# A graph attention kernel: its last stage compares against a row held in PSUM, spreads destinations by one-row products, and reads stored differences

## The chip, the cores and the metric

The kernel runs on one core of a Trainium2 chip. The metric is device time in microseconds (us), median of several executions. A profile is one execution recorded by the hardware profiler; it names the engines PE (TensorE), DVE (VectorE), ACT (ScalarE), POOL (GpSimd) and SP (SyncE, which here only starts transfers). "L1079" means line 1079 of the kernel.

## The reference: two rounds of attention over a graph

There are 3125 nodes with 768 features and 53125 edges, sorted by destination. Each edge has one of three types, and each type has its own weight matrix. A layer multiplies every node by all three matrices, scores every edge from its two ends, takes a softmax over the edges that arrive at one node, and sums the weighted source rows. The first layer has four heads and is followed by an elu, the second has one head. The output is a layer norm of the input plus the second layer.

```python
xr = jnp.einsum('nd,rdf->rnf', x, W)
oi, oj = xr[etype, dst], xr[etype, src]
alpha = jax.nn.leaky_relu(oi @ q + oj @ k, NEG_SLOPE)
m = jax.ops.segment_max(alpha, dst, num_segments=n_nodes)
e = jnp.exp(alpha - m[dst])
z = jax.ops.segment_sum(e, dst, num_segments=n_nodes)
msg = (e / (z[dst] + EPS))[:, :, None] * oj.reshape(-1, heads, out_ch)
out = jax.ops.segment_sum(msg.reshape(-1, heads * out_ch), dst, num_segments=n_nodes)
```

## The kernel before

The nodes are cut into NB = 25 blocks of P = 128. A block's edges lie in SL = 18 slots of 128 edges (nine slots for the last block), so there are NK = 24*18 + 9 = 441 slots. Four pieces of code follow each other:

- `prepare` and the weight work that runs beside it (to about 120 us) write the edge arrays to DRAM. `ed_d` holds, as float32 rows, the source row index, the destination times 2**100 (`BIG`) and the edge type; `dr_d` holds, as bfloat16, the destination's number inside its block. Ahead of and behind the edges, `front` and `pad` fill the arrays with values that belong to no node.
- `phase1` (to about 705 us) computes the first layer's three products for all nodes and, beside them, every edge's attention weight.
- `phase2` (to about 1602 us) gathers and sums the first layer's rows, and computes the second layer's products into the table `ftab`.
- `phase3`, the last stage, is where most of the change lies. It starts gathering at 1606 us and ends the kernel.

Nothing in it is reordered by a scheduler: each engine executes its instructions in the order in which the code issues them. `phase3` has one step `k` per slot. In step `k` the code issues the gather of slot `k`, the sums of slot `k - 29` (`LAG` = 29), then all events planned for step `k` by `when`, then `low(k - 27)` and `high(k - 26)`.

- `gather` (it calls a helper, so its line in the profile is L446) is an indirect DMA that POOL prepares: 128 rows of 772 float32 numbers from `ftab` into one of 36 slots of the tiles `G`. There is nothing else for POOL in this stage until the last 18 slots.
- `high` scales and selects. For about half of the slots (`whole`), DVE makes the matrix `selp` (L1064): it compares the row of numbers 0 to 127 (`row`, in SBUF, `frow` in the profile) with each edge's destination `dl` and multiplies by the edge's weight `p`. For the others ACT writes `H`, the weighted row rounded for the faster product (L1068), and DVE makes the 0/1 matrix `sel` (L1070; in the last 18 slots POOL makes it).
- `low` (L1079), for the slots that are not whole, writes `L`, the part of the weighted row that `H` lost: `L = G * p - H`, all three tensors in SBUF.
- `sums` (L1090) is the PE product that adds a slot to its block's sum.

The weights `p` of a block come from a chain of events in its own and the next block's steps. `a_load` (L964) loads `w`, a window of the destinations, through SP's queue. `a_local` (L969) turns it into the destinations inside the block, `dT`. `a_spread` (L978) copies these along all partitions with 18 PE products of 128 columns against the constant `one`, four to a PSUM bank `bc` (two banks), and `a_spread2` (L984) lets ACT copy each bank to `sT`. `a_q` (L989) compares all 2304 columns of `sT` with the partition's number `col` in one DVE instruction; 18 small products (L1000) then fetch each edge's destination score. In the same event DVE makes `f` (L1003), the difference of neighbouring destinations, which is zero inside a node's edges and hugely negative between nodes; the running maximum (`a_scan`, L1030 and L1032) uses it. `a_alpha` (L1017) adds the score column of the gathered rows, so DVE waits there until the block's last gather has landed. The transposes `pa` (L1024), the scan, an exponential (L1039) and a transpose back (L1043) give `p` (L1048). `phase1` has the same `f` in its own `a_scan`, made by DVE from its own window `w`.

Of the kernel before, what the change touches and what calls it, by code (L numbers as in the profile page):

```python
# [8 lines left out]
F32 = mybir.dt.float32  # L9
F32R = mybir.dt.float32r  # L10
F16 = mybir.dt.float16
BF = mybir.dt.bfloat16
# [8 lines left out]
P = 128  # L21
# [30 lines left out]
def kernel(  # L52
# [41 lines left out]
    keep = ctx.enter_context(tc.tile_pool(name="keep", bufs=1))  # L94
    first_rows = {0: 0, 1: 1, 2: 2, NB - 1: 3}

    ed_d = dram.tile([3, LL], F32, name="ed_d")
    dr_d = dram.tile([1, LL], BF, name="dr_d")
    tab1 = dram.tile([NP * R, RW], F32, name="ftab1")
    tab2 = dram.tile([NP * R, RW], F32, name="ftab2")  # L100
# [69 lines left out]
    def prepare(work, bank, wide, half):  # L170

        def tile_(dt):
            return work.tile([EP, ET], dt, name="e", bufs=6)

        di, si, ti = tile_(I32), tile_(I32), tile_(I32)
        for t, a in ((di, dst), (si, src), (ti, etype)):
            nc.scalar.dma_start(t, a.rearrange("(p t) -> p t", p=EP))
        cnt = work.tile([EP, 32], F32, name="cnt")
        V.memset(cnt, 0.0)
        pad = work.tile([P, 3, BACK // P], F32, name="pad")  # L180
        padb = work.tile([P, BACK // P], BF, name="padb")
        front = work.tile([P, 3, FRONT // P], F32, name="front")
        V.memset(pad, 8192.0 * BIG)
        V.memset(front, -BIG)
        V.memset(padb, 0.0)
        ones = work.tile([EP, 1], F32, name="ones")
        V.memset(ones, 1.0)
        yield

        def store(to, t):  # L190
            G.dma_start(to[FRONT:FRONT + E].rearrange("(p t) -> p t", p=EP), t)

        dB = tile_(F32)
        V.tensor_scalar(dB, di, BIG, None, op0=ALU.mult)
        store(ed_d[1], dB)
        for a, lo_, n in ((front, 0, FRONT), (pad, FRONT + E, BACK)):
            G.dma_start(ed_d[:, lo_:lo_ + n].rearrange("r (p k) -> p r k", p=P), a)
            G.dma_start(dr_d[0, lo_:lo_ + n].rearrange("(p k) -> p k", p=P), padb[:, :n // P])
        blk = tile_(I32)
        V.tensor_single_scalar(blk, di, 7, op=ALU.logical_shift_right)  # L200
        bb, junk, dr = (half[:EP, i * ET:(i + 1) * ET] for i in range(3))
        V.tensor_copy(bb, blk)
        for b in range(NB + 1):
            V.tensor_scalar(junk, bb, float(b), 0.0, op0=ALU.is_lt, op1=ALU.add, accum_out=cnt[:, b:b + 1])
            yield
            if b == 10:
                win = wide[:EP, :ET + P]
                c = ed_d[1:2, FRONT:FRONT + 1]
                G.dma_start(win, bass.AP(tensor=c.tensor, offset=c.offset, ap=[[ET, EP], [1, ET + P]]))
                rx = tile_(F32)  # L210
                V.scalar_tensor_tensor(rx, si, float(R), ti, op0=ALU.mult, op1=ALU.add)
                store(ed_d[0], rx)
                yield
                tf = tile_(F32)
                V.tensor_copy(tf, ti)
                store(ed_d[2], tf)
                yield
                V.tensor_single_scalar(di, di, P - 1, op=ALU.bitwise_and)
                V.tensor_copy(dr, di)
                store(dr_d[0], dr)  # L220
                yield

        junk = tile_(F32)
        V.tensor_tensor(junk, dB, win[:, 1:ET + 1], op=ALU.is_gt)
        V.tensor_reduce(cnt[:, 30:31], junk, AX.X, ALU.add)
        yield
        V.tensor_tensor(junk, dB, win[:, P:ET + P], op=ALU.is_equal)
        V.tensor_reduce(cnt[:, 31:32], junk, AX.X, ALU.add)
        yield
        yield  # L230
        yield
        pc = bank[:, :2 * P]
        T.matmul(pc[:1, :32], ones, cnt, start=True, stop=True)
        cf = work.tile([1, 32], F32, name="cf")
        V.tensor_copy(cf, pc[:1, :32])
        V.tensor_copy(starts, cf)
        yield
        big = work.tile([1, 32], F32, name="big")
        V.tensor_sub(big[:, :NB], cf[:, 1:NB + 1], cf[:, 0:NB])
        V.tensor_scalar(big[:, :NB - 1], big[:, :NB - 1], float(CAP), None, op0=ALU.is_gt)  # L240
        V.tensor_scalar(big[:, NB - 1:NB], big[:, NB - 1:NB], float(SLL * P), None, op0=ALU.is_gt)
        V.tensor_copy(big[:, 30:32], cf[:, 30:32])
        V.memset(big[:, NB:30], 0.0)
        tot = work.tile([1, 1], F32, name="tot")
        V.tensor_reduce(tot, big, AX.X, ALU.add)
        V.tensor_copy(flag, tot)
        yield
# [245 lines left out]
    def phase1(pre, work, psum, wH, wL, qq):  # L493
# [8 lines left out]

        def a_window(b):
            s = st[b]
            s["w"] = work.tile([H1 * SL, 3 * P + 2], F32, name="w", bufs=2)
            nc.sync.dma_start(s["w"], at(ed_d, 1, -P - 1, [[P, SL], [0, H1], [1, 3 * P + 2]], start(b, regs)))

        def a_index(b):
            s = st[b]
# [61 lines left out]

        def a_scan(b):
            s = st[b]
            pa = s["pa"]
            f, F, B = (share[i][:H1 * SL, b % 2 * HW:b % 2 * HW + n] for i, n in
                       ((6, 3 * P + 1), (7, 3 * P), (8, 2 * P)))
            V.tensor_sub(f, s["w"][:, 0:3 * P + 1], s["w"][:, 1:3 * P + 2])
            V.tensor_tensor_scan(F, f[:, 0:3 * P], pa[:H1 * SL, :3 * P], -3e38, op0=ALU.add, op1=ALU.max)
            V.tensor_tensor_scan(B[:, ::-1], f[:, P + 1:3 * P + 1][:, ::-1], F[:, P:3 * P][:, ::-1], -3e38,
                                 op0=ALU.add, op1=ALU.max)  # L580
            s["e"] = work.tile([H1 * SL, P], F32, name="e", bufs=2)
            V.tensor_sub(s["e"], pa[:H1 * SL, P:2 * P], B[:, :P])
            S.activation(s["e"], s["e"], AF.Exp)
# [356 lines left out]
    def phase3(work, psum):  # L940
# [8 lines left out]
            V.memset(t, 0.0)  # L949
        blk = {}  # L950
        st = {}
        one = work.tile([SL, SL, P], BF, name="one", bufs=1)
        V.tensor_copy(one, ident[:SL, :SL, None].to_broadcast([SL, SL, P]))

        def gather(k):
            b, j = divmod(k, SL)
# [2 lines left out]
        def a_load(b):  # L959
            s = blk[b] = {}  # L960
            r0 = start(b, regs)
            s["w"] = work.tile([SL, 3 * P + 2], F32, name="w", bufs=2)
            nc.sync.dma_start(s["w"], at(ed_d, 1, -P - 1, [[P, SL], [1, 3 * P + 2]], r0))

        def a_local(b):

            s = blk[b]
            s["dT"] = work.tile([SL, P], BF, name="dT", bufs=2)
            V.tensor_scalar(s["dT"], s["w"][:, P + 1:2 * P + 1], 1.0 / BIG, -float(P * b), op0=ALU.mult, op1=ALU.add)  # L969
            s["sT"] = work.tile([P, CAP], BF, name="sT", bufs=1)  # L970

        def a_spread(b, i):

            s = blk[b]
            js = range(4 * i, min(4 * i + 4, SL))
            bc = psum.tile([P, 512], F32, name="bc", bufs=2)
            for j in js:
                T.matmul(bc[:, (j - 4 * i) * P:(j - 4 * i + 1) * P], one[:, j, :], s["dT"], start=True, stop=True)  # L978
            s["bc", i] = bc, len(js) * P

        def a_spread2(b, i):
            s = blk[b]
            bc, n = s["bc", i]
            S.copy(s["sT"][:, 4 * i * P:4 * i * P + n], bc[:, :n])  # L984

        def a_q(b):
            s = blk[b]
            sT = s["sT"]
            V.tensor_scalar(sT, sT, col, None, op0=ALU.is_equal)  # L989
            s["oh"] = work.tile([P, SL, R * 3], F32, name="oh", bufs=2)  # L990
            V.tensor_tensor(s["oh"], rel[:, b, :, None].to_broadcast([P, SL, R * 3]),
                            rel3.rearrange("p r s -> p (r s)")[:, None, :].to_broadcast([P, SL, R * 3]),
                            op=ALU.is_equal)

        def a_q2(b):
# [3 lines left out]
            for j in range(SL):  # L999
                T.matmul(pq[:, j * nq:(j + 1) * nq], s["sT"][:, j * P:(j + 1) * P],  # L1000
                         q2s[:, b].rearrange("p r s -> p (r s)"), start=True, stop=True)
            s["f"] = work.tile([SL, 3 * P + 1], F32, name="f", bufs=2)
            V.tensor_sub(s["f"], s["w"][:, 0:3 * P + 1], s["w"][:, 1:3 * P + 2])  # L1003

        def a_q3(b):
            s = blk[b]
# [47 lines left out]
        def late(k):  # L1054

            return k >= NK - SL

        def high(k):
# [2 lines left out]
            p = blk[b]["p"][:, j:j + 1]  # L1061
            if whole(k):
                sel = work.tile([P, P], F32, name="selp", bufs=4)
                V.tensor_scalar(sel, row, dl[:, b, j:j + 1], p, op0=ALU.is_equal, op1=ALU.mult)  # L1064
                st[k] = [sel, g]
                return
            H = work.tile([P, RW], F32R, name="H", bufs=4)
            S.activation(H, g, AF.Copy, scale=p)  # L1068
            sel = work.tile([P, P], F32R, name="sel", bufs=4)
            (G if late(k) else V).tensor_scalar(sel, row, dl[:, b, j:j + 1], None, op0=ALU.is_equal)  # L1070
            st[k] = [sel, H]

        def low(k):
# [63 lines left out]
        LAG = SL + 11  # L1137
        for b in range(NB):
            when(max(b * SL - 12, 0), a_load, b)
            when(max(b * SL - 8, 1), a_local, b)  # L1140
            for i in range(5):
                when(max(b * SL - 4, 2) + 2 * i, a_spread, b, i)
                when(max(b * SL - 4, 2) + 1 + 2 * i, a_spread2, b, i)
# [601 lines left out]
```

## Time and profile before

| | |
|---|---|
| Median of 3 executions | 2298.87 us (2294.52 to 2303.71) |
| The profiled execution | 2300.63 us, of which the span is 2298.8 us |
| PE, DVE, ACT, POOL busy, share of the span | 89%, 71%, 54%, 76% |
| Last stage, 1606 to 2250 us: PE, DVE, ACT, POOL busy | 551.79, 459.18, 321.64, 509.36 of 644 us |
| Granted PE clock and mean DMA share there | 0.91, 0.85 |
| End of the last stage, 2250 to 2299 us: PE, DVE, ACT, POOL busy | 31.48, 31.73, 17.35, 11.66 of 49 us |

Busy time on POOL counts the gather instructions, not the short gaps between them, and a matmul's end is modelled, so a busy PE isn't a PE at its peak. In the lists of groups, a line gives the line of the kernel, the engine, the operation, the tiles (written <- read), shapes and types, how often, then the busy time in us and the mean of one in ns, then the engine's idle time just before it and what ended that.

### The profile page before, as it was taken

How to read it: one execution, taken by the hardware profiler on the slowest of the kernel's cores; microseconds unless marked ns; L12 is line 12 of the kernel's file. 1: busy time of each engine (PE TensorE's matmuls, PEld its weight loads, DVE VectorE, ACT ScalarE, POOL GpSimd, SP SyncE). 2: the span in 40 equal slices, each digit the busy share in tenths (PEclk: the TensorE clock that was granted, in tenths of full speed). 3: DMA queues.
4: the chain of work that ended last, by engine and by line, in shares of the span. 5: the costliest groups of instructions: out<-in, count | busy, mean ns of one | idle time of the engine just before them, and what ended most of it. 6: DMA issues, size and time to landing. Idle time of an engine off the chain costs nothing.

```text
span 2298.8 us, 37986 instructions
## 1 busy us (share of the span) xinstructions
PE 2050.6 (89%) x11380; PEld 1774.1 (77%) x11380; DVE 1635.4 (71%) x4349; ACT 1231.3 (54%) x2745; POOL 1751.9 (76%) x1684
## 2 busy tenths in 40 slices
PE   6998978988995899999999999998598898899886
PEld 5888878888885799999999999998355555565554
DVE  7734434434433999999999999994477777777776
ACT  5411111211111888888888888884255554555553
POOL 4167777777776888888888888883777777777773
PEclk9999998999998999999999999999698999999997
DMA  6554544444465977777777777775888888888881
GB/s 174 179 164 148 175 138 155 162 163 146 150 201 169 318 243 230 233 229 240 236 232 234 234 232 234 238 229 194 288 286 275 288 291 285 286 264 289 272 272 65
DMA packets 153482, 507.92 MB, mean 221 GB/s; under 512 B 40362, under 2 KB 53697, under 8 KB 153269
## 3 DMA queue, kind: packets, MB, share of 16 engines
q0 software_dynamic: 85408, 333.97, 47.9%
q1 hardware_dynamic: 57631, 155.46, 18.8%
q10 hardware_dynamic: 10230, 15.98, 2.1%
q8 instruction: 94, 1.54, 0.3%
q14 instruction: 119, 0.97, 0.1%
HBM read 428.29 MB, written 93.81 MB: 227 GB/s over the span
## 4 chain that ended last, share of the span: by engine, by line
PE 42%; POOL 7%; DVE 6%; DMA 6%; issue 5%; ACT 1%; POOLq 0%; DVEq 0%; ACTq 0%
PE acc L1090 15%; PE po L873 14%; PE acc L818 11%; DMA G<-ftab,ridx 4%; POOL share L446 3%; POOL sel L787 2%; DVE L L799 2%; POOL G L446 1%; DVE L L1079 1%; PE bc L978 1%; DMA G<-ftab,rfirst 1%; ACT H L785 1%; PE pt L848 1%; DMA share<-ftab,rfirst 1%; PE pa L1024 0%
## 5 line engine op out<-in xcount | busy, mean ns | idle before, releaser
L785 ACT ACTIVATE H<-share,pall 128x193 fp32r<-128x193 f32 x1748 | 643.1, 447 | 105.3 <-DMA share<-ftab,ridx 46.8
L799 DVE SCALAR_TENSOR_TENSOR L<-share,pall,H 128x193 fp32r<-128x193 f32 x1748 | 648.1, 436 | 25.8 <-ACT H L785 14.1
L873 PE MATMUL po<-wH,hT 128*128 128x386 f32 (+1 forms) x1800 | 533.1, 339 | 0.0
L446 POOL DMA_INDIRECT G<-ftab,ridx x378 | 439.0, 1161 | 115.2 <-issue 58.2
L446 POOL DMA_INDIRECT kt<-kt,ridx x378 | 404.0, 1069 | 115.2 <-issue 113.9
L446 POOL DMA_INDIRECT share<-ftab,ridx x378 | 429.3, 1136 | 81.4 <-DVE L L799 42.0
L626 PE MATMUL po<-wH,xT 128*128 128x384 f32 x1584 | 444.4, 353 | 0.1
L1090 PE MATMUL acc<-G,selp 128*128 128x386 f32 x904 | 359.8, 524 | 1.0 <-DVE selp L1064 1.0
L873 PEld LDWEIGHTS po<-wH,hT 128*128 128x128 f32 x1800 | 334.6, 189 | 0.6 <-DVE hT L861 0.5
L873 PE MATMUL po<-wL,hT 128*128 128x386 f32 (+1 forms) x900 | 305.1, 339 | 0.0
L626 PEld LDWEIGHTS po<-wH,xT 128*128 128x128 f32 x1584 | 301.5, 196 | 2.7 <-DVE xT L613 0.3
L626 PE MATMUL po<-wL,xT 128*128 128x384 f32 x792 | 275.3, 348 | 0.0
L818 PE MATMUL acc<-H,sel 128*128 128x386 f32 x874 | 242.0, 358 | 20.2 <-POOL sel L787 10.3
L638 ACT COPY share<-po 128x384 f32<-128x384 f32 x144 | 69.0, 479 | 326.7 <-PE po L626 267.1
L787 POOL TENSOR_SCALAR sel<-frow,fdl 128x128 fp32r<-128x128 f32 x291 | 224.8, 773 | 12.9 <-PE acc L818 1.1
L1079 DVE SCALAR_TENSOR_TENSOR L<-G,p,H 128x772 fp32r<-128x772 f32 x215 | 217.7, 1013 | 22.2 <-ACT H L1068 19.8
L1090 PEld LDWEIGHTS acc<-G,selp 128*128 128x128 f32 x904 | 172.4, 202 | 78.4 <-issue 11.2
L818 PE MATMUL acc<-L,sel 128*128 128x386 f32 x874 | 226.3, 340 | 0.0
L1068 ACT ACTIVATE H<-G,p 128x772 fp32r<-128x772 f32 x215 | 195.0, 934 | 44.7 <-issue 35.1
L818 PEld LDWEIGHTS acc<-H,sel 128*128 128x128 f32 x874 | 149.1, 189 | 56.0 <-POOL sel L787 47.2
L560 DVE TENSOR_TENSOR a<-qe,kt 128x72 f32<-128x72 f32 x25 | 5.8, 233 | 241.1 <-DMA kt<-kt,ridx 205.7
L873 PEld LDWEIGHTS po<-wL,hT 128*128 128x128 f32 x900 | 169.7, 189 | 0.0
(230 smaller groups left out, 2926.3 us busy)
## 6 DMA issues: line engine op xcount, KB each, us to landing
ftab<-r SPq DMA_DIRECT2D x75, 386.0 KB
ftab<-share SPq DMA_DIRECT2D x72, 386.0 KB
sT<-dr_d SPq DMA_DIRECT2D x25, 576.0 KB
share<-in_L_gnn_W_dram SPq DMA_DIRECT2D x36, 384.0 KB
w_d<-w2hl SPq DMA_DIRECT2D x18, 768.0 KB
share<-in_x_dram SPq DMA_DIRECT2D x25, 384.0 KB
xb_d<-share SPq DMA_DIRECT2D x25, 384.0 KB
xr<-in_x_dram SPq DMA_DIRECT2D x23, 384.0 KB
```

The lines of the kernel that those rows point to most:

```text
L446: G.indirect_dma_start(out=to, out_offset=None, in_=tab, in_offset=_index(i[:, j:j + 1]), bounds_check=NP * R - 1, oob_is_err=False)
L626: T.matmul(po[:, :HALF], xT[:, s, t, :], w[:, i, sl], start=(n == 0), stop=(n == 3 * DT - 1))
L638: S.copy(to, po[:, :HALF].rearrange("p (h f) -> p h f", h=2))
L785: S.activation(H[:, c], g[:, c], AF.Copy, scale=pall[:, b, j, h:h + 1])
L787: (V if k % 3 == 0 else G).tensor_scalar(sel, row, dl[:, b, j:j + 1], None, op0=ALU.is_equal)
L799: V.scalar_tensor_tensor(L[:, c], g[:, c], pall[:, b, j, h:h + 1], H[:, c].bitcast(F32), op0=ALU.mult, op1=ALU.subtract)
L818: T.matmul(acc[:, c, :HW], sel, a[:, c * HW:(c + 1) * HW], start=(j == 0 and i == 0), stop=(k in ends2 and i == 1), skip_group_check=True)
L848: T.transpose(pt[:, t // 3, (t % 3) * P:(t % 3 + 1) * P], s["ey"][:, t * P:(t + 1) * P], ident)
L873: T.matmul(po[:, :wd], hT[:, k, t, :], w[:, r * DT + t, sl], start=(t == 0 and n == 0), stop=(t == DT - 1 and n == 2))
L1068: S.activation(H, g, AF.Copy, scale=p)
L1079: V.scalar_tensor_tensor(L, g, blk[b]["p"][:, j:j + 1], st[k][1].bitcast(F32), op0=ALU.mult, op1=ALU.subtract)
L1090: T.matmul(acc[:, c, :HW], sel, a[:, c * HW:(c + 1) * HW], start=(j == 0 and i == 0), stop=(k in ends and i == len(parts) - 1))
```

## The change

- `ed_d` gets a fourth row. At the end of `prepare` DVE subtracts each destination from its predecessor in one instruction over 125 partitions of 425 numbers, and POOL stores the result `df` there. `pad` and `front` grow by a row.
- `phase1` and `phase3` load the window of that row as `f` and no longer subtract.
- In `phase3` `a_load` also loads the block's 2304 numbers of `dr_d` as one row `d` on one partition; `w`, `dT` and `a_local` are gone. `one` is a single row of 128 ones.
- `a_spread` is one product of up to 512 columns for each bank (five for a block), with a contraction over one row. `bc` has one bank instead of two.
- `a_spread2` is now a DVE instruction that reads the bank, compares with `col` and writes the result to `sT`. The compare over 2304 columns in `a_q` is gone.
- `rowp`, a copy of `row`, takes the PSUM bank that `bc` gave up. DVE's `selp` and `sel` compare with `rowp`; POOL's `sel` of the last slots still compares with `row`.

```diff
-    ed_d = dram.tile([3, LL], F32, name="ed_d")
+    ed_d = dram.tile([4, LL], F32, name="ed_d")
...
+        df = tile_(F32)
+        V.tensor_sub(df, dB, win[:, 1:ET + 1])
+        store(ed_d[3], df)
...
-            s["w"] = work.tile([H1 * SL, 3 * P + 2], F32, name="w", bufs=2)
-            nc.sync.dma_start(s["w"], at(ed_d, 1, -P - 1, [[P, SL], [0, H1], [1, 3 * P + 2]], start(b, regs)))
+            s["f"] = work.tile([H1 * SL, 3 * P + 1], F32, name="w", bufs=2)
+            nc.sync.dma_start(s["f"], at(ed_d, 3, -P - 1, [[P, SL], [0, H1], [1, 3 * P + 1]], start(b, regs)))
...
-            V.tensor_sub(f, s["w"][:, 0:3 * P + 1], s["w"][:, 1:3 * P + 2])
...
-        one = work.tile([SL, SL, P], BF, name="one", bufs=1)
-        V.tensor_copy(one, ident[:SL, :SL, None].to_broadcast([SL, SL, P]))
+        one = work.tile([1, P], BF, name="one", bufs=1)
+        V.memset(one, 1.0)
+
+        rowp = psum.tile([P, 512], F32, name="rowp", bufs=1)[:, :P]
+        V.tensor_copy(rowp, row)
...
-            s["w"] = work.tile([SL, 3 * P + 2], F32, name="w", bufs=2)
-            nc.sync.dma_start(s["w"], at(ed_d, 1, -P - 1, [[P, SL], [1, 3 * P + 2]], r0))
-
-        def a_local(b):
-
-            s = blk[b]
-            s["dT"] = work.tile([SL, P], BF, name="dT", bufs=2)
-            V.tensor_scalar(s["dT"], s["w"][:, P + 1:2 * P + 1], 1.0 / BIG, -float(P * b), op0=ALU.mult, op1=ALU.add)
-            s["sT"] = work.tile([P, CAP], BF, name="sT", bufs=1)
+            s["f"] = work.tile([SL, 3 * P + 1], F32, name="f", bufs=2)
+            nc.sync.dma_start(s["f"], at(ed_d, 3, -P - 1, [[P, SL], [1, 3 * P + 1]], r0))
+            s["d"] = work.tile([1, CAP], BF, name="d", bufs=2)
+            nc.sync.dma_start(s["d"], at(dr_d, 0, 0, [[CAP, 1], [1, CAP]], r0))
...
-            js = range(4 * i, min(4 * i + 4, SL))
-            bc = psum.tile([P, 512], F32, name="bc", bufs=2)
-            for j in js:
-                T.matmul(bc[:, (j - 4 * i) * P:(j - 4 * i + 1) * P], one[:, j, :], s["dT"], start=True, stop=True)
-            s["bc", i] = bc, len(js) * P
+            if i == 0:
+                s["sT"] = work.tile([P, CAP], BF, name="sT", bufs=1)
+            n = min(4, SL - 4 * i) * P
+            bc = psum.tile([P, 512], F32, name="bc", bufs=1)
+            T.matmul(bc[:, :n], one, s["d"][:, 4 * i * P:4 * i * P + n], start=True, stop=True)
+            s["bc", i] = bc, n
...
-            S.copy(s["sT"][:, 4 * i * P:4 * i * P + n], bc[:, :n])
+            V.tensor_scalar(s["sT"][:, 4 * i * P:4 * i * P + n], bc[:, :n], col, None, op0=ALU.is_equal)
...
-            V.tensor_scalar(sT, sT, col, None, op0=ALU.is_equal)
...
-            s["f"] = work.tile([SL, 3 * P + 1], F32, name="f", bufs=2)
-            V.tensor_sub(s["f"], s["w"][:, 0:3 * P + 1], s["w"][:, 1:3 * P + 2])
...
-                V.tensor_scalar(sel, row, dl[:, b, j:j + 1], p, op0=ALU.is_equal, op1=ALU.mult)
+                V.tensor_scalar(sel, rowp, dl[:, b, j:j + 1], p, op0=ALU.is_equal, op1=ALU.mult)
...
-            (G if late(k) else V).tensor_scalar(sel, row, dl[:, b, j:j + 1], None, op0=ALU.is_equal)
+            if late(k):
+                G.tensor_scalar(sel, row, dl[:, b, j:j + 1], None, op0=ALU.is_equal)
+            else:
+                V.tensor_scalar(sel, rowp, dl[:, b, j:j + 1], None, op0=ALU.is_equal)
...
-            when(max(b * SL - 8, 1), a_local, b)
```

## The prediction

> **What bounds the kernel now.** I read the busy slices, then the last stage by windows, its groups, its waits, and POOL and DVE in order of time. Three windows, 300 us from the middle of the last stage:
>
> ```profile
> core 0: us, PE busy (x) PEld busy (x) DVE busy (x) ACT busy (x) POOL busy (x), PEclk, DMA share, GB/s
> 1850.00:1950.00 100.00, 91.45 (x440) 58.31 (x438) 76.67 (x193) 52.07 (x71) 79.28 (x69) 0.95 0.86 286
> 1950.00:2050.00 100.00, 91.61 (x447) 58.65 (x445) 79.24 (x199) 55.78 (x75) 78.97 (x70) 0.97 0.85 279
> 2050.00:2150.00 100.00, 88.30 (x421) 56.33 (x420) 74.76 (x187) 49.57 (x67) 78.97 (x70) 0.93 0.85 277
> ```
>
> PE is the busiest (90%), POOL stands at 79%. The groups of the same 300 us:
>
> ```profile
> L446 POOL DMA_INDIRECT G<-ftab,ridx x207 | 239.4, 1156 | 63.1 <-issue 31.4 <-PE acc L1090 9.1 <-DMA G<-ftab,ridx 5.5
> L1079 DVE SCALAR_TENSOR_TENSOR L<-G,p,H 128x772 fp32r<-128x772 f32 x100 | 101.3, 1013 | 6.7 <-ACT H L1068 6.6
> L1064 DVE TENSOR_SCALAR selp<-frow,fdl,p 128x128 f32<-128x128 f32 x108 | 36.5, 340 | 0.0
> L1070 DVE TENSOR_SCALAR sel<-frow,fdl 128x128 fp32r<-128x128 f32 x101 | 28.6, 283 | 0.0
> L978 PE MATMUL bc<-dT,one 18*128 18x128 bf16 x204 | 21.7, 222 | 0.0
> L989 DVE TENSOR_SCALAR sT<-sT,fcol 128x2304 bf16<-128x2304 bf16 x12 | 9.6, 801 | 0.0
> L1003 DVE TENSOR_TENSOR f<-w 18x385 f32<-18x385 f32 x12 | 6.5, 540 | 0.0
> L1017 DVE TENSOR_TENSOR a<-qe,G 128x6 f32<-128x6 f32 x33 | 4.5, 165 | 51.4 <-DMA G<-ftab,ridx 51.4
> L969 DVE TENSOR_SCALAR dT<-w 18x128 bf16<-18x128 f32 x12 | 2.5, 208 | 0.0
> L1035 DVE TENSOR_TENSOR e<-pa,B 18x128 f32<-18x128 f32 x12 | 3.3, 278 | 0.4
> ```
>
> POOL's gathers fill the time: 239.4 busy + 63.1 before them = 302.5 us. The 63.1 is 207 gaps of 0.30 us, whoever is named as their ender; between 1606 and 2250 us no gather waited longer. A gather may overwrite its buffer once the slot 36 earlier has been summed; matching gathers to sums in order of time, that sum ended 7 to 16 us earlier (median 11). So **POOL paces the stage**: 441 gathers take 643.45 us (1606.15 to 2249.60), 26.4 us for a block of 18, and DVE idles 51.4 us of 300 in L1017, waiting for them. The chain of waits names PE most because it follows the last releaser; PE, too, idles at the block's transposes, until L1017 is through.
>
> What makes a gather long is seen in the timeline, POOL first:
>
> ```profile
> 1770.96 1.01 POOL L446 DMA_INDIRECT G<-ftab,ridx  x1 [0.30 <-DVE sel L1070]
> 1772.28 2.24 POOL L446 DMA_INDIRECT G<-ftab,ridx  x1 [0.30 <-PE pa L1043]
> 1774.83 1.66 POOL L446 DMA_INDIRECT G<-ftab,ridx  x1 [0.31 <-DVE sel L1070]
> ...
> 1772.17 0.54 DVE L1003 TENSOR_TENSOR f<-w 18x385 f32<-18x385 f32 x1
> 1772.63 1.00 DVE L1079 SCALAR_TENSOR_TENSOR L<-G,p,H 128x772 fp32r<-128x772 f32 x1
> 1773.57 0.33 DVE L1064 TENSOR_SCALAR selp<-frow,fdl,p 128x128 f32<-128x128 f32 x1
> ...
> 1774.59 1.02 DVE L1079 SCALAR_TENSOR_TENSOR L<-G,p,H 128x772 fp32r<-128x772 f32 x1
> ```
>
> An undisturbed gather takes 1.01 us. The one at 1774.83 starts inside an L1079 that ends at 1775.61, and ends 0.88 us after that. The one at 1772.28 starts inside L1003, which L1079 follows at once, and ends 0.89 us after L1079. I noted for all 441 gathers which DVE instruction was running as they started. Their time over 1.009 us sums to 64.4 us. 166 starts inside an L1079 hold 52.0 of it, and "0.885 us after L1079's end, or 1.009" reproduces 44.7; the other 7.1 come with an L989 that runs near the gather's end (2190.39: 2.13 us, ending 0.13 us after an L989). Starts inside L1003 hold 3.4, two starts ahead of L1003 most of the 4.4 noted at L1070, the scan L1032 3.1; L1064 holds 0.6.
>
> **The change part by part.** Sums against this execution: span 2298.8, its own time 2300.63; the median shown, 2298.87, lies 1.76 below that, so I apply differences to the median.
>
> *Gathers, removed.* L1003 and L989 are gone, and with a PSUM operand L1064 and L1070 should stop counting: 3.4 + 4.4 + 7.1 + 0.6 = **-15.5 us**. L1079, the bulk, is untouched. Here a rule of the Trainium skill is to be weighed ("SBUF — State Buffer", Who interferes with whom): a DVE instruction in a 2-port mode, or with two SBUF inputs against a GpSimd instruction that reads SBUF, shuts GpSimd out for its whole length. Taken as "selections in SBUF block POOL", it would give up to the whole 64.4. The rows say the second half of the rule is the one at work (G and H are both in SBUF), and that the selections, 0.3 us each, end too soon to matter. I take the rows.
>
> *Gathers, moved.* Delay depends on how long L1079 still runs. A delayed gather and its successor keep step with DVE's cycle of L1079 + selp + sel, so a longer cycle meets the next gather with a later end. 79 of the starts had 0.12 to 0.40 us of L1079 left; all of them later by the two selections' lengthening (0.132, below) is 10.4; 41 more with 0.70 to 0.85 left would make 16, if none falls out at the far end. The other bound is a gain of a few us, if steps fall apart favourably. I take half of 10.4: **+5**.
>
> *DVE, selections.* Losing a double rate on 128 numbers is like having 64 more. L1003 takes 540 ns for 385 numbers, L1008 310 for 162, so a number at single rate is 1.03 ns, and 64 are 66: L1070 goes from 283 to 349, L1064 from 340 to 406, 18 x 0.066 = 1.2 us per block. L1035, 278 for 128 with a PSUM operand, fits: it has no pointer scalar to read. The skill speaks against this ("VectorE: DVE Perf Modes", Why PSUM operands drop a tier, and The TRN2 errata): PSUM operands lose the double rate, and its table adds 62 cycles of fixed cost, 131 ns in all (an estimate from that page), or 2.4 us per block. This trace shows no such fixed cost (a one-column read of PSUM takes 142 ns at L1097, of SBUF 154 at L1112), so I take the row and keep 2.4 for the range.
>
> *DVE, compares.* Five PSUM reads per block, from L1101's 1018 ns for 768 numbers from PSUM: 1018 - 256 x 1.03 = 754 for 512 columns, 490 for 256: 4 x 0.754 + 0.49 = 3.5, less 0.07 overlap each, 3.15. Removed: L989 0.74, L1003 0.48, L969 0.13 = 1.35 (same overlap taken off). Net +1.8.
>
> *DVE, new wait.* `a_spread2` now waits for PE. Behind it in DVE's order are the step's `low` and `high`, for which PE waits in turn. Placing each L978 end against the DVE select ahead of the new instruction: PE is done before in 72%, mean positive wait 0.19 us, five per block: 1.0; DVE will come later than now, so 0.5. The `bc` bank, single now, is free in time in all cases.
>
> *DVE together.* 26.4 - 4.5 (L1017's wait: 51.4 over 11.4 blocks) = 21.9 used now; + 1.2 + 1.8 + 0.5 - 0.3 (waits for H, since ACT drops five copies, 2.7 us, and its wait for `bc`) = **25.1 per block**. POOL's new pace is 18 x (643.45-10.5)/441 = 25.8. DVE's slack pays, with 0.7 left; no time on the path.
>
> *PE.* 18 products (x8 take 1.01 us in the timeline: 0.126 each, 2.3) become 5 wider ones, bounded by four times 0.126 each: 0 to 2.3, so 0 to 2.2 less, take 1. It is not the pace: nothing.
>
> *SP, prepare, phase1.* The load of `d` joins SP's queue behind `f`, eight steps (11 us) ahead of its use, where `w` had four; nothing. The subtraction in `prepare` is some 0.6 us of DVE, one POOL store 0.7 (L375's), in a stretch where POOL is 30% busy: 0 to 1, take 0. `phase1` is PE's stage (513 of 580 us busy); 25 fewer subtractions there hide: 0. The start at 1606.15 waits for the last `ftab` store, as before.
>
> *The end.* After the last gather 49 us follow on PE and DVE; some 15 selections lie in it: 15 x 0.066 = **+1**.
>
> Sum: -15.5 + 5 + 1 = -9.5, **2289 us**.
>
> **The rivals.**
> (a) *The selections do hold POOL*, or the phases fall well: half to nearly all of the 64.4 goes and PE stays under 25 a block: -20 to -60, 2240 to 2279. For: L1064 follows nearly every L1079. Against: a start inside L1032, with DVE idle behind it, is delayed alike.
> (b) *DVE becomes the pace*, slower. At the page's price for PSUM (+1.2 per block) with the full wait for `bc` (+0.5) DVE needs 26.8 per block; it decides from 26.4 on. At 26.8: 24.5 x 0.4 + 1 = +11; with compares 0.15 longer each too, 27.5: +28: 2310 to 2327. For: only 0.7 us slack. Against: the rows' prices.
> (c) *Nothing happens*: as many gathers meet L1079 as escape L989: within 3 us.
>
> **How the numbers follow.** Mine 0.45, its own range 2280 to 2300; (a) 0.20; (b) 0.28; (c) 0.07. About 0.5% (11.5 us) is what a measurement here can tell from no change. Mine lies 2 us inside it and splits 0.20 faster, 0.25 same; so faster 0.40, same 0.32, slower 0.28. The range, 2262 to 2318, cuts the ends of (a) and (b).
>
> **What would show it.** Right: gathers' mean from 1.156 towards 1.13, gaps still 0.30, maxima of 2.2 us gone; selections at 349 and 406 ns; L1017's wait down from 4.5 to about 1 us per block. Wrong: gaps in POOL over 0.30 (then DVE or PE paces), selections over 420 ns, or the gather mean at 1.05 (then they were the lock).

## The result, and the profile after

The changed kernel takes 2291.15 us (median of 7 executions, 2284.13 to 2298.96) against 2299.23 us before (median of 7, 2294.52 to 2303.71). The ratio is 0.9963, 95% interval 0.9940 to 0.9986: a gain of 0.37%, which is real and smaller than the 0.5% that was taken as the bound. On a second chip the same two kernels gave 2296.04 and 2302.91 us, ratio 0.9964 (0.9948 to 0.9981). The forecast was 2289.

The profiled execution took 2296.29 us, its span is 2294.5. The same three windows of the last stage:

```profile
1850.00:1950.00 100.00, 91.85 (x390) 56.30 (x389) 85.65 (x200) 45.41 (x54) 79.28 (x69) 0.95 0.87 287
1950.00:2050.00 100.00, 90.01 (x384) 55.52 (x385) 87.95 (x203) 44.32 (x54) 78.66 (x71) 0.95 0.86 283
2050.00:2150.00 100.00, 90.97 (x387) 55.89 (x387) 86.93 (x200) 43.30 (x52) 78.96 (x70) 0.95 0.85 280
```

In the order of the columns, PE and POOL are where they were, DVE went from 77% to 87%, ACT from 52% to 44%. The groups of these 300 us that answer to those shown before (L moved to L1080, selp to L1062, sel to L1071, the spread to L980 and L986, the score addition to L1015):

```profile
L451 POOL DMA_INDIRECT G<-ftab,ridx x208 | 237.9, 1144 | 63.4 <-issue 30.5 <-PE acc L1091 8.2 <-DMA G<-ftab,ridx 5.5
L1080 DVE SCALAR_TENSOR_TENSOR L<-G,p,H 128x772 fp32r<-128x772 f32 x101 | 102.2, 1012 | 0.0
L1062 DVE TENSOR_SCALAR selp<-rowp,fdl,p 128x128 f32<-128x128 f32 x109 | 43.5, 401 | 0.0
L1071 DVE TENSOR_SCALAR sel<-rowp,fdl 128x128 fp32r<-128x128 f32 x101 | 34.2, 339 | 0.0
L986 DVE TENSOR_SCALAR sT<-bc,fcol 128x512 bf16<-128x512 f32 x45 | 33.5, 744 | 0.0
L980 PE MATMUL bc<-d,one 1*128 1x512 bf16 x46 | 17.6, 383 | 1.1 <-DVE sT L986 1.1
L986 DVE TENSOR_SCALAR sT<-bc,fcol 128x256 bf16<-128x256 f32 x12 | 5.5, 462 | 0.0
L1015 DVE TENSOR_TENSOR a<-qe,G 128x6 f32<-128x6 f32 x33 | 4.8, 174 | 32.3 <-DMA G<-ftab,ridx 30.5 <-issue 1.8
L980 PE MATMUL bc<-d,one 1*128 1x256 bf16 x12 | 4.0, 338 | 0.9 <-DVE sT L986 0.9
```

The gathers' mean went from 1156 to 1144 ns and the gaps ahead of them are still 0.30 us each (63.4 for 208); the largest gap of the stage is 0.311 us. POOL still sets the pace. DVE's wait at the score addition (L1015) went from 51.4 to 32.3 us of the 300. The selections cost 401 and 339 ns instead of 340 and 283, the compares 744 and 462. None of the three groups has idle time in front of it: DVE never waits for the spread products in these windows. They did not become cheaper either: 17.6 + 4.0 us busy against 21.7.

Where the 4.3 us between the two spans lie, from the starts and ends of the gathers: the stage's first gather starts 4.0 us later (1610.11 against 1606.15); the 441 gathers, gaps included, take 636.34 instead of 643.45 us, 7.1 less; what follows the last takes 48.06 instead of 49.24, 1.2 less. Of the first, 1.4 us are there when the first layer's products end (705.4 against 704.0) and the rest comes in `phase2`, whose code is the same. Five profiles of kernels that share all code up to the last stage start it between 1607.1 and 1612.1 us, so most of it looks like scatter; but all five start later than the one profile of the kernel before, and a cost of a few us ahead of the stage is not excluded.

Repeating the exercise of the prediction, with the DVE instruction that ran 45 ns ahead of each start: the gathers' time over 1.009 us each, called the excess from here on, sums to 57.2 us, before to 64.4. Of that, 137 starts inside an L hold 54.0 us, and "0.885 us after L's end, or 1.009" gives 55.0 for them (counted so, the kernel before has 162 such starts, 52.9 us, and 45.4 by the rule). The starts inside selections hold 0.1 us in sum, those inside compares of `sT` 0.3. A place in the order of time, POOL first:

```profile
2241.99 1.00 POOL L451 DMA_INDIRECT G<-ftab,rfirst  x1 [0.31 <-issue]
2243.30 1.83 POOL L451 DMA_INDIRECT G<-ftab,rfirst  x1 [0.30 <-DVE sel L1071]
...
2242.36 0.46 DVE L986 TENSOR_SCALAR sT<-bc,fcol 128x256 bf16<-128x256 f32 x1
2242.75 0.33 DVE L1071 TENSOR_SCALAR sel<-rowp,fdl 128x128 fp32r<-128x128 f32 x1
2243.01 0.31 DVE L991 TENSOR_TENSOR oh<-rel,rel 128x162 f32<-128x162 f32 x1
2243.24 1.00 DVE L1080 SCALAR_TENSOR_TENSOR L<-G,p,H 128x772 fp32r<-128x772 f32 x1
```

The gather at 2241.99 runs beside a compare and a selection and takes 1.00 us. The one at 2243.30 starts inside an L that ends at 2244.24, and ends 0.89 us after it. The gathers of over 2 us are gone (11 before, none after; longest 1.835; none in the profile of the repeat on the second chip either).

### The profile page after: what moved, and what is told of

Same layout as the page of the kernel before. It is cut to its first block, busy times and chain, and to the rows that moved or that the text cites. A ratio compares the mean times of both kernels' runs of the same rounds, so it can differ in the third digit from the quotient of the medians.

```text
span 2294.5 us, 37251 instructions
## 1 busy us (share of the span) xinstructions
PE 2047.2 (89%) x11055; PEld 1758.8 (77%) x11055; DVE 1685.4 (73%) x4377; ACT 1172.9 (51%) x2620; POOL 1749.5 (76%) x1685
## 4 chain that ended last, share of the span: by engine, by line
PE 35%; DVE 14%; POOL 7%; issue 6%; DMA 5%; ACT 1%; POOLq 0%; DVEq 0%; ACTq 0%
PE po L876 15%; PE acc L821 11%; PE acc L1091 7%; DMA G<-ftab,ridx 4%; DVE L L1080 4%; POOL share L451 3%; POOL sel L790 2%; DVE selp L1062 1%; DVE L L802 1%; DVE sT L986 1%; POOL G L451 1%; DVE sel L1071 1%; DMA G<-ftab,rfirst 1%; PE pt L851 1%; DVE stats L1109 1%
## 5 line engine op out<-in xcount | busy, mean ns | idle before, releaser
L451 POOL DMA_INDIRECT G<-ftab,ridx x378 | 432.5, 1144 | 115.2 <-issue 54.0
L1080 DVE SCALAR_TENSOR_TENSOR L<-G,p,H 128x772 fp32r<-128x772 f32 x215 | 217.5, 1013 | 1.4 <-issue 0.7
L1066 ACT ACTIVATE H<-G,p 128x772 fp32r<-128x772 f32 x215 | 189.8, 927 | 47.5 <-issue 34.0
```

Source lines behind the costliest of these rows:

```text
L451: G.indirect_dma_start(out=to, out_offset=None, in_=tab, in_offset=_index(i[:, j:j + 1]), bounds_check=NP * R - 1, oob_is_err=False)
L1080: V.scalar_tensor_tensor(L, g, blk[b]["p"][:, j:j + 1], st[k][1].bitcast(F32), op0=ALU.mult, op1=ALU.subtract)
```

## The experiments

Theory: POOL paces the last stage; its gathers are held by L, which has two tensor inputs in SBUF; the change takes away the holds of the subtraction and of the large compare, and gives some of that back because longer DVE steps shift the starts. Rivals: the selections in SBUF held POOL, so the PSUM row is what gained; DVE has become the pace.

Twelve runs were made on three chips. One of them (the changed kernel's repeat, the second run of the selections put back, the operand moved, the added instruction) behaves like the chip of the first measurement. On the two others the granted clock of TensorE is lower. One line of the windows shows it, the 580 us of the first layer's products, first in the changed kernel on the first chip, then in an experiment on a slower one:

```profile
120.00:700.00 580.00, 512.97 (x3165) 492.16 (x3166) 233.25 (x514) 104.74 (x204) 449.19 (x419) 0.95 0.49 162
```

```profile
120.00:700.00 580.00, 456.39 (x2503) 416.08 (x2502) 190.29 (x419) 83.44 (x164) 365.40 (x345) 0.86 0.39 126
```

There the last of these products ends at 889 us instead of 705, the whole kernel takes 2506 and 2530 us before the change, and in the last stage POOL waits at times, often for PE (gaps up to 8 us). The lower clock is not the whole of it: from 200 to 600 us a product with `wH` takes 374 instead of 353 ns, 6% more, and in the 580 us PE stops 65 times for over 0.5 us where it stopped 23 times. What makes it stop is not shown. Times on those two chips say little about POOL; the excess of the gathers is read there as everywhere, since it does not count the gaps. It has scatter of its own: the two profiles of the changed kernel, both at the usual clock, differ by 4.2 us (57.2 and 61.4), and those of the selections put back, one at each clock, by 3.6. The kernel before was timed beside every run, but it has one profile, from the first chip.

**One operand moved: does L hold the gathers?**

```diff
-            V.scalar_tensor_tensor(L, g, blk[b]["p"][:, j:j + 1], st[k][1].bitcast(F32), op0=ALU.mult, op1=ALU.subtract)
+            V.scalar_tensor_tensor(L, g, blk[b]["p"][:, j:j + 1], rowp[:, 0:1].to_broadcast([P, RW]), op0=ALU.mult, op1=ALU.subtract)
```

> The changed kernel with one operand moved: L is made as G * p minus one PSUM number instead of minus H, so L has a single SBUF tensor input and the subtraction of H is left out (the output is another). Count, shape and order of all instructions stay. My theory: L is what holds the gathers, so the excess over 1.009 us falls from 57 to 5 or less, a gather's mean to about 1.01 us, and POOL needs 23.7 us per block; DVE then is about level with it, so the time falls by 35 to 50 us, not by more. Rival (the selections or something else hold POOL, or the delay comes from DMA traffic): excess 40 or more, time within 10 us of the changed kernel.

Measured: 2238.38 us, 57.7 less than the changed kernel on the same chip; ratio to the kernel before 0.9720 (0.9699 to 0.9741). The excess is 1.3 us. Groups of POOL and DVE (POOL from 1620 to 2180 us, DVE from 1850 to 2150):

```profile
L451 POOL DMA_INDIRECT G<-ftab,ridx x378 | 382.3, 1011 | 115.8 <-issue 46.6 <-DMA G<-ftab,ridx 13.1 <-PE acc L1091 11.6
```

```profile
L1080 DVE SCALAR_TENSOR_TENSOR L<-G,p,rowp 128x772 fp32r<-128x772 f32 x110 | 110.7, 1006 | 0.0
```

L takes the same time (1006 against 1012 ns) and comes in the same place, only its second operand isn't in SBUF, and the mean gather falls to 1011 ns. One thing more differs: L no longer waits for ACT's `H`, but it had no idle time in front of it in the changed kernel either (0.0 us above). This settles that L holds the gathers, and that POOL paces the stage: the stage's gathers take 580.92 us instead of 640.48, and the kernel gains nearly all of it. It gained more than expected, because DVE was not level with POOL: it was busy 94% in these windows, 22.4 us of 23.7 per block. DMA traffic, named as a rival, is out as well: it is denser here (the DMA engines are 90 to 92% busy in the three windows, 85 to 87% in the changed kernel), and the gathers are not slowed by it.

That it is the second SBUF input, and not L's length, can be seen in the kernel before without any edit. L1101 takes 1018 ns, as long as L, but one of its tensor inputs is in PSUM (`acc`). The scan L1030 (`F`, 936 ns) reads PSUM too; the scan L1032 (`B`, 0.68 us) has both inputs in SBUF. In order of time, POOL first in each pair:

```profile
1860.76 1.01 POOL L446 DMA_INDIRECT G<-ftab,ridx  x1 [0.30 <-issue]
1860.12 1.02 DVE L1101 SCALAR_TENSOR_TENSOR share<-acc,rz,share 128x768 f32<-128x768 f32 x1
...
1953.15 1.37 POOL L446 DMA_INDIRECT G<-ftab,ridx  x1 [0.30 <-PE bc L978]
1953.02 0.68 DVE L1032 TENSOR_TENSOR_SCAN B<-f,F 18x256 f32<-18x256 f32 x1
```

Of the 22 gathers of the stage that start inside an L1101 and the 11 that start inside an L1030, none takes over 1.012 us; the 12 that start inside an L1032 hold 3.1 us.

**An instruction added: how much room has DVE?**

```diff
                 V.tensor_scalar(sel, rowp, dl[:, b, j:j + 1], None, op0=ALU.is_equal)
+                spare = work.tile([P, 3 * P], F32, name="spare", bufs=1)
+                V.tensor_scalar(spare.rearrange("p (a c) -> p a c", a=3), rowp[:, None, :].to_broadcast([P, 3, P]),
+                                dl[:, b, j:j + 1], None, op0=ALU.is_equal)
```

> The changed kernel with one more DVE instruction in every slot that is not whole: a compare of 384 numbers from PSUM into a scratch tile, some 0.55 us each, 4.7 us per block. My theory: DVE's slack in the changed kernel is its wait at the score addition, 2.65 us per block; so the first 2.65 are free and the rest, 2.0 us x 24, is paid: 40 to 60 us slower than the changed kernel, that wait near zero, and gaps of more than 0.31 us between gathers, because POOL now waits for buffers. Rival (DVE is already the pace in the changed kernel): the full 4.7 x 24 = 113 us. Rival (PE or POOL has all the say): less than 15 us.

Measured: 2318.11 us, 22.1 over the changed kernel on that chip; ratio to before 1.0064 (1.0046 to 1.0082). Between expectation and last rival. The sums of the three windows, the changed kernel's repeat first and then this one (PE, weight load, DVE, ACT, POOL busy, then their means):

```profile
sum 300.00, PE 272.45 PEld 167.90 DVE 256.59 ACT 132.01 POOL 237.51; mean PE 90.82 PEld 55.97 DVE 85.53 ACT 44.00 POOL 79.17
```

```profile
sum 300.00, PE 265.89 PEld 155.91 DVE 296.40 ACT 126.69 POOL 239.15; mean PE 88.63 PEld 51.97 DVE 98.80 ACT 42.23 POOL 79.72
```

DVE is now full: no wait is left; it is busy 26.7 us per block where it was busy 22.4. The size was wrong because I had counted only the wait at the score addition as room; all of DVE's idle time was room, 43 of 300 us, 3.8 us per block. And the way was partly wrong: gaps between gathers stayed at 0.305 us. The cost shows as gathers held more often (176 starts inside an L instead of 136; excess 77.1 against 61.4, 15.7 us) and a longer end (51.9 against 48.0 us). The 36 buffers hide how far DVE has fallen behind: through the stage an L starts on average 41 to 45 us after its slot's gather, where it was 38 to 40, and is still done at least 6 us before the buffer is filled again. So DVE is not the pace of the changed kernel, and would be with some 4 us more per block.

**The three parts, each alone on the kernel before.** First the selections:

```diff
+        rowp = psum.tile([P, 512], F32, name="rowp", bufs=1)[:, :P]
+        V.tensor_copy(rowp, row)
...
-            bc = psum.tile([P, 512], F32, name="bc", bufs=2)
+            bc = psum.tile([P, 512], F32, name="bc", bufs=1)
...
-                V.tensor_scalar(sel, row, dl[:, b, j:j + 1], p, op0=ALU.is_equal, op1=ALU.mult)
+                V.tensor_scalar(sel, rowp, dl[:, b, j:j + 1], p, op0=ALU.is_equal, op1=ALU.mult)
...
-            (G if late(k) else V).tensor_scalar(sel, row, dl[:, b, j:j + 1], None, op0=ALU.is_equal)
+            (G if late(k) else V).tensor_scalar(sel, row if late(k) else rowp, dl[:, b, j:j + 1], None, op0=ALU.is_equal)
```

> The kernel before with one part of the change alone: DVE's selections compare with a copy of the row in PSUM (and the spread products have one bank instead of two, to make room). My theory: the selections never held POOL, so what the gathers lose over 1.009 us each (64.4 us in all before) loses only 0.6 us directly and gains 5 to 10 us because DVE's cycle of L, selp and sel is longer; selections 339 and 401 ns as in the changed kernel; time 2300 to 2308. Rival (the selections in SBUF are the lock): the excess falls by 10 us or more, time 2289 or less.

> The kernel before with the PSUM selections alone, a second time, hoped for on a chip that grants TensorE its usual clock. My theory, after the first run (excess 84.9 instead of 64.4, no time difference on the slower chip): the longer selections raise the excess to 70 to 85 us and the time by 5 to 15 us over the kernel before. Rival (the selections in SBUF are the lock): excess 55 or less, time 5 us or more below before.

Both runs fell on slower chips. Ratio to before 0.9999 (0.9971 to 1.0027) and 0.9983 (0.9948 to 1.0017): no difference in time. The excess is 84.9 and 79.3 us (the second from the longest of its executions), against 64.4 in the kernel before on its own chip. The mean gather from 1620 to 2180 us in the first of them:

```profile
L446 POOL DMA_INDIRECT G<-ftab,ridx x223 | 269.8, 1210 | 73.5 <-issue 49.4 <-PE acc L1092 9.4 <-DMA G<-ftab,ridx 4.9
```

The rival is out: the excess did not fall with the selections' place. It rose by 15 to 20 us, more than the scatter above; how much of that is the chip's is not known, as the kernel before has no profile there. Starts inside L hold 67.1 and 62.9 us (before 52.9), and the subtraction's neighbours some 8 us more. That the time doesn't show it is no proof that it costs nothing, since PE sets part of the pace on these chips.

Second, the stored differences (the window `w` is still loaded, for the destinations; the same in `phase1`, where the window of the differences takes the place of `w`):

```diff
+            s["f"] = work.tile([SL, 3 * P + 1], F32, name="f", bufs=2)
+            nc.sync.dma_start(s["f"], at(ed_d, 3, -P - 1, [[P, SL], [1, 3 * P + 1]], r0))
...
-            s["f"] = work.tile([SL, 3 * P + 1], F32, name="f", bufs=2)
-            V.tensor_sub(s["f"], s["w"][:, 0:3 * P + 1], s["w"][:, 1:3 * P + 2])
```

> The kernel before with the stored differences alone: row 3 of ed_d is written once, both stages load it and subtract no more (the window w is still loaded as well, for the destinations). My theory: the gathers that started inside or just ahead of the subtraction lose their delay, 3.4 + 2.7 = 6 us, so the excess goes from 64.4 to about 58 and the time to about 2293; no gather over 2.2 us is left except those that end with the large compare. Rival (the subtraction was hidden): excess within 3 us of 64.4, time within 3 us of before.

Excess 59.7 us (from an execution of 2517 us, where the median is 2501), near the 58 expected, but the 4.7 us below 64.4 are no more than the scatter; ratio 1.0006 (0.9977 to 1.0035) on a slower chip, so the time neither shows nor excludes the 6 us. One gather of 3.04 us is left: it starts 0.11 us ahead of the large compare, and the hold runs through that, the small compare `oh` and an L.

Third, the spreading (here `f` has one buffer, for room):

```diff
-                T.matmul(bc[:, (j - 4 * i) * P:(j - 4 * i + 1) * P], one[:, j, :], s["dT"], start=True, stop=True)
+            T.matmul(bc[:, :n], one, s["d"][:, 4 * i * P:4 * i * P + n], start=True, stop=True)
...
-            S.copy(s["sT"][:, 4 * i * P:4 * i * P + n], bc[:, :n])
+            V.tensor_scalar(s["sT"][:, 4 * i * P:4 * i * P + n], bc[:, :n], col, None, op0=ALU.is_equal)
...
-            V.tensor_scalar(sT, sT, col, None, op0=ALU.is_equal)
```

> The kernel before with the new spreading alone: destinations loaded as one row, one-row products, DVE compares five PSUM banks instead of one 2304-column compare in SBUF; the differences are still made by DVE in the stage, the selections stay in SBUF. My theory: the 7.1 us that gathers lost to the large compare go, and 1 us more at starts ahead of it; some 3 us come back because DVE's steps with a compare are longer; excess about 59, time about 2294, DVE never waits for the products. Rival (DVE's compares wait for PE and become the pace): gaps over 0.31 us between gathers, time 2305 or more.

Excess 63.1, four above the expectation and hardly below 64.4; ratio 1.0000 (0.9962 to 1.0037). The starts inside an L hold 54.5 us here. That what the large compare had held came back as longer holds by L would fit, but at this scatter it is not shown. Gaps were over 0.31 us and DVE did wait for PE at times, but so it is with every kernel on that chip, so this run does not decide on the rival; the waits view of the changed kernel's repeat, on a chip like the first, does (its last line for DVE in the 300 us):

```profile
DVE sT L986 <- PE bc L980: 0.4, 1, 0.4
```

**The changed kernel with the selections back in SBUF.**

```diff
-                V.tensor_scalar(sel, rowp, dl[:, b, j:j + 1], p, op0=ALU.is_equal, op1=ALU.mult)
+                V.tensor_scalar(sel, row, dl[:, b, j:j + 1], p, op0=ALU.is_equal, op1=ALU.mult)
...
-                V.tensor_scalar(sel, rowp, dl[:, b, j:j + 1], None, op0=ALU.is_equal)
+                V.tensor_scalar(sel, row, dl[:, b, j:j + 1], None, op0=ALU.is_equal)
```

> The changed kernel with the selections back in SBUF, so differences and spreading without the PSUM row. My theory: the PSUM row costs and does not help, so the excess falls from 57.2 to about 50, the wait of DVE for the gathers at the score addition rises from 2.65 to about 3.8 us per block, time about 2284, 5 to 8 below the changed kernel. Rival (the PSUM row is what gains): excess 64 or more, time 2296 or more.

> The changed kernel once more, beside the kernels below on one chip. The four runs so far were on a chip that grants TensorE a lower clock (0.92 against 0.95) and takes 9% longer. My theory: as in the first measurement, gathers' excess over 1.009 us near 57 us, and a time 0.3 to 0.5% below the kernel before.

> The changed kernel with the selections back in SBUF, measured a second time, now beside the changed kernel itself. My theory: as the longer selections move the starts of the gathers to where L has longer to run, this one is 3 to 8 us faster than the changed kernel (excess near 50 to 55). The first run of it showed an excess of 60.2, which speaks for no difference. Rival (the PSUM row gains): it is 5 us or more slower than the changed kernel.

On the slower chip: excess 60.2 (expected 50), ratio to before 0.9912 (0.9880 to 0.9944). That is some 22 us, where its two parts alone gave nothing on that chip (1.0006 and 1.0000) and the excess is no lower than theirs; where these 22 us come from is not known. On the chip with the changed kernel beside it: 2291.59 us against 2296.04, ratios to before 0.9944 (0.9929 to 0.9958) and 0.9964 (0.9948 to 0.9981); excess 56.6 against 61.4. The two intervals overlap. Time and excess differ by 4.5 and 4.8 us in the direction of the theory, but the other pair of profiles differs the other way (60.2 against 57.2). So the rival of a gain of 5 us by the PSUM row is out, and whether the row costs anything is not resolved. The version with the selections in SBUF has the lowest median of the complete ones on a chip like the first, by a margin that is not separated.

**Fewer L, and shorter ones.** If L's holds are the cost, two other edits must reduce it: more slots that need no L, and L in two halves of 386 columns with the slot's selection between them, the latter in both forms of the selection.

```diff
-WHOLE = (13, 25)
+WHOLE = (15, 25)
```

> The changed kernel with 15 of 25 slots whole instead of 13, so 176 or so instead of 215 L instructions. My theory: the gathers' excess goes with the number of L, 18% fewer, so from 57 to 61 down to about 48, time 8 to 12 us below the changed kernel; PE gets 0.4 us more per block and has room. Rival (PE has no room): gaps of more than 0.31 us between gathers, time equal to the changed kernel or above.

```diff
-            V.scalar_tensor_tensor(L, g, blk[b]["p"][:, j:j + 1], st[k][1].bitcast(F32), op0=ALU.mult, op1=ALU.subtract)
+            V.scalar_tensor_tensor(L[:, w], g[:, w], blk[b]["p"][:, j:j + 1], H[:, w].bitcast(F32), op0=ALU.mult, op1=ALU.subtract)
...
             if 0 <= k - LAG + 2 < NK:
-                low(k - LAG + 2)
+                low(k - LAG + 2, 0)
             if 0 <= k - LAG + 3 < NK:
                 high(k - LAG + 3)
+            if 0 <= k - LAG + 2 < NK:
+                low(k - LAG + 2, 1)
```

> The changed kernel with each L made in two instructions of 386 columns, the slot's selection (which reads PSUM) between them. My theory: the lock is held for one instruction, so a gather that starts in one waits for at most 0.55 us instead of 1.0; with starts spread evenly the mean loss per gather falls from 0.13 to 0.06 us, the excess from 57 to about 28; DVE gets some 1.2 us per block more and has 3.8 (its share idle in the changed kernel, 14.5% of 26.2 us); time 20 to 30 us below the changed kernel. Rival (DVE's added time counts): time equal to the changed kernel or above.

> The same split with the selections back in SBUF. It tells whether a selection in its faster SBUF form lets POOL in between the halves as the PSUM form does. My theory: the delay counts from the end of the instruction that ran when the gather started, whatever follows, so this is as good or a few us better (excess 20 to 28, time 20 to 35 below the changed kernel). Rival (the SBUF selection holds the port as well and joins the two halves to one hold of 1.3 us): excess 55 or more, time no better than the changed kernel.

All three ran on a slower chip, where the kernel before takes 2530.15 us.

| | excess, us | ratio to the kernel before |
|---|---|---|
| changed kernel, first chip and repeat | 57.2, 61.4 | 0.9963, 0.9964 |
| 15 of 25 whole | 37.8 | 0.9921 (0.9894 to 0.9947) |
| L in halves, selections in PSUM | 34.6 | 0.9954 (0.9925 to 0.9982) |
| L in halves, selections in SBUF | 45.5 | 0.9963 (0.9936 to 0.9990) |

The excess fell in all three, by more than the scatter, though the changed kernel itself has no run on this chip. The times, forecast 8 to 35 us below the changed kernel's, can't be judged for the same reason; the ratios of the halves, 0.9954 and 0.9963, cannot be told from the changed kernel's on the other chips. With fewer L the excess fell by more than their number did (from 137 to 91 starts inside an L). With halves in PSUM form it came near the forecast of 28. With the selections in SBUF I had expected 20 to 28, and 45.5 is a miss: in several places a hold now runs through both halves and the selection between them:

```profile
2005.10 2.65 POOL L451 DMA_INDIRECT G<-ftab,ridx  x1 [0.31 <-issue]
...
2005.15 0.31 DVE L989 TENSOR_TENSOR oh<-rel,rel 128x162 f32<-128x162 f32 x1
2005.38 0.60 DVE L1081 SCALAR_TENSOR_TENSOR L<-G,p,H 128x386 fp32r<-128x386 f32 x1
2005.91 0.33 DVE L1060 TENSOR_SCALAR selp<-frow,fdl,p 128x128 f32<-128x128 f32 x1
2006.17 0.60 DVE L1081 SCALAR_TENSOR_TENSOR L<-G,p,H 128x386 fp32r<-128x386 f32 x1
```

The second half ends at 2006.77, the gather at 2007.75, 0.98 us later. There are four such gathers (2.65 to 2.71 us). With the selection in PSUM no gather is held through both halves (longest 1.85 us). So the rival of that run looks right in such places: an SBUF selection can join its neighbours to one hold. How much of any of this a chip at the usual clock turns into time was not measured: on this one POOL's gaps reach 8 us and average 0.42 to 0.43 us instead of 0.305.

## Why the prediction was right

**What bounds the kernel.** POOL, held by L: shown by the moved operand, 57.7 us, and by L1101, which is as long, has one input in PSUM and holds nothing. The rule that the prediction weighed speaks of 2-port selections and of instructions with two SBUF inputs alike; the choice for the second half of it stands. The selections alone moved to PSUM did not lower the excess.

**Gathers, removed: -15.5 forecast.** Measured from the two profiles: what isn't a start inside L fell from 11.5 to 3.3 us, and what L's starts hold beyond the 0.885 rule fell from 7.4 to -1.1. That is 16.7 together.

**Gathers, moved: +5 forecast.** By the rule, L's starts rose from 45.4 to 55.0: +9.6. The sign and the cause are as forecast, the size was near the upper one of the bounds that I halved. The two net to 7.1 us less, where 10.5 was said. The repeat's profile gives -13.8 and +10.8, a net of only 3.0. So the two terms are seen twice with their signs; their difference, which is the gain, is no larger than the scatter of single profiles.

**DVE.** Selections 401 and 339 ns (forecast 406 and 349), compares 744 and 462 (754 and 490): the rows were right, and the page's higher price for PSUM was not paid (131 ns more by the prediction's estimate from it; measured 56 and 61). The sum, 25.1 us per block, was not: DVE is busy 260.5 us for 208 gathers, which is 22.5. Two terms made the difference. The base of 21.9 took every idle stretch but one as work (busy were 230.7 us for 207 gathers, 20.1); and the new wait for PE, taken at 0.5, is about zero. A slip of 0.1 is in it too: 441 gathers in 643.45 us are 26.3 us per block, not 26.4. So the room was 3.4 to 3.8 us and not 0.7, and the wait at the score addition fell to 2.8 us per block and not to about 1. This did not touch the forecast, since DVE is off the path either way, but it made rival (b) look far likelier than it was: DVE had to be given 4.3 us more per block for the time to rise by 22.

**PE.** Taken at 1 us less per block, the spread products take nothing less (21.6 against 21.7 us in 300). Off the path.

**The end: +1 forecast,** -1.2 in the profile (48.06 against 49.24 us; 48.03 in the repeat's). Small either way.

So 2289 against 2291 has terms in it that were off by 1 to 5 us. The median fell by 8.1 us, while the two profiled spans differ by 4.3, so the sum can't be checked term by term to better than a few us; that it came within 2 us is partly luck. That the gain is small because L is untouched is not.

## What to carry to other kernels

An engine whose busy time reads 79% can be the pace: look for gaps of constant length and for buffers that were free long before. When such an engine's instructions come in two lengths, sort them by what its neighbour was doing as they started, before believing which neighbour is at fault; moving one operand of the suspect is then a cheap proof. And the room that an engine has is all its idle time, not the one wait that is easiest to see.

## What was not expected of the hardware

- Two instructions with two SBUF inputs differ in how they pass a hold on. After L alone a held gather ends 0.885 us behind L, whatever follows (0.88 to 0.89 for eight in ten of them in both profiles of the changed kernel). When a small two-input subtraction or compare (L1003 before; `oh`, L989 with L in halves) stands directly ahead of L, the hold runs through both, and it did so for gathers that had started 0.08 us ahead of the subtraction: seven of them took 2.44 us each in the first run of the selections alone. Why these, and not starts 0.01 to 0.1 us ahead of an L by itself, is left open.
- The gathers fall into step with DVE: a held one ends at a fixed distance from L's end, so the next meets the next L at a fixed point. Removing one hold would therefore shift all others. It would explain why the spreading alone, which takes away 7 us of holds, left the excess at 63.1, but that was not tested by itself.
- On two of the three chips of the experiments TensorE has a granted clock of 0.83 to 0.88 from 120 to 700 us, where it has 0.95 on the third and on the chip of the first measurement; the kernel before takes 2506 and 2530 us there instead of 2299 and 2303. Whether the clock makes PE stop more often there, or PE's stops the lower clock, is open.
